# The last pair of step 0: keys and queries made ahead of the products with U, and one buffer for keys and values in both steps

## Chip, cores and metric

The kernel runs on one core of one Trainium2 chip. Its metric is the device time of one execution in microseconds (us), given as the median over several executions. A core has TensorE (PE; its weight loads are shown apart as PEld), VectorE (DVE), ScalarE (ACT), GpSimd (POOL) and SyncE (SP). In this kernel SP only starts transfers, and POOL starts some as well.

## The reference, cut to what matters

There are two layers over N = 2708 rows of D = 512 numbers. The first is graph attention with a dense adjacency matrix. The second spreads features in two steps, and in each step forms an attention matrix that keeps, in each row, the largest entries up to a share of 0.9 of the mass (the nucleus). The change is in the second layer:

```python
def _adj_from_feats(Xa, W1, W2, W3):
    Q = Xa @ W1
    K = Xa @ W3
    logits = Q @ W2 @ K.T / TAU
    ...                                  # keep the nucleus of each row
    return jax.nn.softmax(masked, axis=1)
Xf, Xb, Xa = (X, X, X)
Z = jnp.zeros_like(X)
for s in range(STEPS):                   # STEPS = 2
    A = _adj_from_feats(Xa, W1, W2, W3)
    Xf = Rf @ Xf
    Xb = Rb @ Xb
    Xa = A @ Xa
    Z = Z + (Xf @ U1[s] + Xb @ U2[s] + Xa @ U3[s])
Y = X + Z                                # then a layernorm
```

Step 1 can form no row of its attention before it has keys for every row of the Xa that step 0 made: its keys need the whole of step 0's attention, but nothing of Z, and so nothing of the products with U.

## The kernel before, in words

Rows are cut into 22 tiles of 128 (the last has 20), and tiles are worked in 11 pairs. The first layer fills the time up to about 1074 us, where its last projection ends. Then comes `for s in range(STEPS)`, which opens its pools of buffers anew for each step.

For one pair a step does this. `Logits.products` (L517) multiplies queries with keys, and ACT copies the result out (`p`, L519). ACT takes exponentials, and `search` finds the cut of each row on DVE with passes over whole rows (`L624`, `L800`, `L802`). `attended` turns the kept entries (L1004), copies them (`at`, L1008) and multiplies them with the values `va` (L1023); the result, scaled, is `xa` (L1031). `mixed` then forms the pair's share of Z. It turns the rows of xf, xb and xa (`transposed`, L147, copied to `v_t` by L149) and multiplies them with U1, U2 and U3, in this order, all into two PSUM tiles (L1051). Each of U's twelve pieces `u_k` is loaded by SP (L1049) into three buffers in step 0, so the load of one piece waits for the product three pieces earlier. In step 0 `mixed` calls `project` last: 16 small matmuls (L160) with `kw` give keys and queries of the next step. ACT copies them (L165, L166), POOL splits them in a high and a low part (L170 to L172) and stores them in `kq_d` (L173). At the very end `mixed` adds up Z: ACT copies (`yo`, L1064), POOL adds the old rows (L1068) and stores to `y_d` (L1070).

Between the products of a pair, PE also multiplies pieces of the graph matrix (`part`, L959, with the loads `hl` and `s_r`), so that PE has something to do while DVE searches. For the last pair of a step no such pieces are left.

A step begins with SP loading `keys` from `kq_d` (L924, two loads of 2560 columns and two of 148), then in step 1 `g_b` (L933), and then the queries `q_t` of the first two pairs (L505). Step 1 then calls `ranks`: DVE makes a ramp in a buffer named `s_r` (L1098), PE multiplies it with `keys` (L1103), ACT copies the result to `same` (L1104), PE turns that (L1108), ACT copies columns out (`own`, L1112), and DVE counts with it (L1119). Only then come the first logits of step 1 (L517).

The order of the work on PE, ACT, DVE and SP within a step's main part is written out by hand (`tc.manual_schedule`). The loads of keys and of `g_b` stand outside that part; there a scheduler decides where in SP's queue they go. [...] A pool that is opened where an older one was released makes the first user of its memory wait until the whole older pool is done with:

```python
        with ExitStack() as st:
            big = st.enter_context(tc.tile_pool(name=f"s{s}big", bufs=1))
            ...
            va = big.tile([P, NT, D], F32, name="va")

            keys = big.tile([P, N], F32R, name="keys")
```

Of the kernel before, what the change touches and what calls it, by code (L numbers as in the profile page):

```python
# [9 lines left out]
F32 = mybir.dt.float32  # L10
BF16 = mybir.dt.bfloat16
# [13 lines left out]
P = 128  # L25
# [28 lines left out]
def kernel(  # L54
# [100 lines left out]
    def project(pool, pk, v_t, t, s):  # L155


        pr = rows[t]
        for k in range(KD):
            nc.tensor.matmul(pk[:, :pr], lhsT=kw[:, k, :], rhs=v_t[:, k, :pr], start=(k == 0), stop=(k == KD - 1))  # L160
        big = pool.tile([P, P], F32, name="kq_b")
        hl = pool.tile([P, 2, P], F32, name="kq_hl")
        if pr < P:
            nc.gpsimd.memset(hl, 0.0)
        nc.scalar.copy(hl[:, 1, :pr], pk[:, :pr])  # L165
        nc.scalar.mul(big[:, :pr], pk[:, :pr], 4097.0)  # L166


        high, x = hl[:, 0, :pr], hl[:, 1, :pr]
        nc.gpsimd.tensor_tensor(high, big[:, :pr], x, op=OP.subtract)  # L170
        nc.gpsimd.tensor_tensor(high, big[:, :pr], high, op=OP.subtract)
        nc.gpsimd.tensor_tensor(x, x, high, op=OP.subtract)  # L172
        nc.gpsimd.dma_start(out=kq_d[s][:, :, t * P:(t + 1) * P], in_=hl)  # L173
# [419 lines left out]
    def search(lg, looked, early, late):  # L593
# [307 lines left out]
        v.reciprocal(rden, den)  # L901
        return keep, rden

    for s in range(STEPS):
        last = s == STEPS - 1
        with ExitStack() as st:
            big = st.enter_context(tc.tile_pool(name=f"s{s}big", bufs=1))
            wide = st.enter_context(tc.tile_pool(name=f"s{s}wide", bufs=2))
            sp = st.enter_context(tc.tile_pool(name=f"s{s}sp", bufs=4 if last else 3))
            work = st.enter_context(tc.tile_pool(name=f"s{s}work", bufs=2))  # L910
            up = st.enter_context(tc.tile_pool(name=f"s{s}u", bufs=4))
            parts = None if last else st.enter_context(tc.tile_pool(name=f"s{s}parts", bufs=2))
            small = st.enter_context(tc.tile_pool(name=f"s{s}small", bufs=2))
            ps_t = st.enter_context(tc.tile_pool(name=f"s{s}pst", bufs=2, space=PSUM))
            ps_a = st.enter_context(tc.tile_pool(name=f"s{s}psa", bufs=2, space=PSUM))
            ps_s = st.enter_context(tc.tile_pool(name=f"s{s}pss", bufs=1, space=PSUM))

            va = big.tile([P, NT, D], F32, name="va")

            keys = big.tile([P, N], F32R, name="keys")  # L920
            h = (NT - NT % G - G) * P
            for c in (slice(0, h), slice(h, N)):
                for i in range(2):
                    nc.sync.dma_start(out=keys[i * DA:(i + 1) * DA, c].bitcast(F32), in_=kq_d[s][:DA, i, c])  # L924
            rank = big.tile([P, N], BF16, name="rank") if last else None

            def values():
                for t in range(NT):
                    nc.sync.dma_start(out=va[:rows[t], t, :], in_=(xa_d if last else va_d)[cols[t], :])

            if last:
                g_b = big.tile([P, D], F32, name="g_b")
                nc.sync.dma_start(out=g_b, in_=row_bcast(gamma, D))  # L933

            def part(half, b):
# [101 lines left out]
            def turned_rows(grp, v):  # L1037
                return [transposed(up, ps_t, v[i], rows[t], "v_t") for i, t in enumerate(grp)]

            def mixed(grp, v_t, xb, xa, others, fills):  # L1040

                pz = [ps_a.tile([P, D], F32, name="a") for _ in grp]
                for n, u in enumerate((u1, u2, u3)):
                    nxt = turned_rows(grp, (xb, xa)[n]) if n < 2 else None
                    for k in range(KD):
                        u_k = up.tile([P, D], F32, name="u_k", bufs=4 if last else 3)
                        nc.sync.dma_start(out=u_k, in_=u[s, k * P:(k + 1) * P, :])  # L1049
                        for i, t in enumerate(grp):  # L1050
                            nc.tensor.matmul(pz[i][:rows[t]], lhsT=v_t[i][:, k, :rows[t]], rhs=u_k,  # L1051
                                             start=(n == 0 and k == 0), stop=(n == 2 and k == KD - 1))
                        paced(others, 1)
                        if n < 2 and k < 3:
                            paced(fills, 1)
                    if n == 2 and not last:
                        for i, t in enumerate(grp):
                            project(small, ps_t.tile([P, 512], F32, name="t"), v_t[i], t, s + 1)
                    v_t = nxt
                out_ = []  # L1060
                for i, t in enumerate(grp):
                    pr = rows[t]
                    y = work.tile([P, D], F32, name="yo")
                    nc.scalar.copy(y[:pr], pz[i][:pr])  # L1064
                    z = work.tile([P, D], F32, name="xw", bufs=2) if last else va[:, t, :]
                    if last:
                        nc.sync.dma_start(out=z[:pr], in_=y_d[cols[t], :])
                    nc.gpsimd.tensor_tensor(y[:pr], y[:pr], z[:pr], op=OP.add)  # L1068
                    if not last:
                        nc.gpsimd.dma_start(out=y_d[cols[t], :], in_=y[:pr])  # L1070
                    out_.append((t, y))
                return out_
# [66 lines left out]
            with tc.manual_schedule(engines={PE, ACT, DVE, SP}):  # L1139
                counted, spread = ranks() if last else (None, None)  # L1140
                lg = [Logits(pools, s, grp, keys, rank) for grp in pairs[:1]]
                lg[0].queries()
                lg[0].products()
                steps = lg[0].exp(looks=False)
                if last:
                    counted()
                for step in steps:
                    step()
                half = []
                lg += [Logits(pools, s, grp, keys, rank) for grp in pairs[1:2]]  # L1150
                lg[1].queries()
                for step in part(half, 0):
                    step()
                values()
                done = []
                ready = None
                looks, left = [], []
                for g in range(-1, NP):

                    fills = []  # L1160
                    if g + 2 < NP:
                        lg[g + 2].products()
                    paced(looks, len(looks))
                    if g + 3 < NP:
                        lg.append(Logits(pools, s, pairs[g + 3], keys, rank))
                        lg[g + 3].queries()
                    norms = [normed(t, y) for t, y in done] if last else []
                    done = []

                    rows_in = []  # L1170
                    if g >= 0:
                        left.append(lambda g=g: rows_in.extend(diffused(pairs[g])))
                    others = left + part(half, g + 2)
                    left = []

                    def early(g=g):
                        if g + 2 < NP:
                            fills.extend(lg[g + 2].exp())
                        return lambda: [rest() for rest in norms]

                    def late(g=g):
                        if g >= 0:
                            keep, rden = ready
                            if g:
                                paced(others, 1)
                            xa, v_t = attended(pairs[g], keep, rden, fills, others, lambda: turned_rows(pairs[g], rows_in[0]))
                            done.extend(mixed(pairs[g], v_t, rows_in[1], xa, others, fills))
                            paced(others, len(others))
                            paced(fills, len(fills))
                            return  # L1190


                        if last:
                            spread()
                        paced(fills, 5 + G * NA)
                        paced(others, NT if last else NT - NT // 2)
                        looks.extend(fills)
                        left.extend(others)

                    if g + 1 < NP:  # L1200
                        ready = search(lg[g + 1], g >= 0, early, late)
                    else:
                        for rest in norms:
                            rest()
                        late()
                if last:
                    for rest in [normed(t, y) for t, y in done]:
                        rest()
# [31 lines left out]
```

## Time and profile before

| | us |
|---|---|
| median of 3 runs (3777.3 to 3778.19) | 3777.57 |
| time of the profiled execution | 3774.21 |
| its span, first to last instruction | 3772.1 |
| PE busy | 3383.3 (90%) |
| DVE busy | 2611.1 (69%) |
| ACT busy | 1540.1 (41%) |
| POOL busy | 838.2 (22%) |
| last product with U in step 0 (L1051) ends | 2321.6 |
| first product with the keys of step 1 (L1103) begins | 2338.98 |

The profile is one execution, so times within it are compared with its own span; 2.1 us lie around that span, and the median of the runs shown is 3.4 us over the profiled execution's time. Matmuls overlap and their ends are modelled, so a busy PE isn't yet a PE at its peak. An fp32 product is recorded as two matmuls here: 48 records are the 24 products of one pair with U. A wait for several things is put down to the one that came last.

### The profile page before, as it was taken

Reading aid. Unit: us, or ns where it says so; the run is one execution under the profiler, and the core shown is the slowest. Engines: PE = TensorE matmul, PEld = TensorE weight load, DVE = VectorE, ACT = ScalarE, POOL = GpSimd, SP = SyncE. Lnnn points to the kernel's source line nnn. Section 1 sums busy time; section 2 is a strip of 40 time slices with the busy share of each in tenths; the row PEclk is TensorE's granted clock in tenths of the full one; section 3 lists DMA queues with packets and bytes.
Section 4 is the critical chain, followed back from the end, with each engine's and each line's share of the span. In section 5 each row is a group of like instructions: output and inputs, shape, how many; then the busy total and the mean of one; then the engine's idle time right before and its main releaser. Section 6 shows DMA issues by size and latency. Waiting matters only on the chain. (4 is left out here: it accounts for less than half of the span.)

```text
span 3772.1 us, 35425 instructions
## 1 busy us (share of the span) xinstructions
PE 3383.3 (90%) x11143; PEld 1760.6 (47%) x11143; DVE 2611.1 (69%) x4814; ACT 1540.1 (41%) x2334; POOL 838.2 (22%) x1187
## 2 busy tenths in 40 slices
PE   8999999999855898989898998668999999999988
PEld 4433333333533455545454453435555665556443
DVE  4588888989946526474554641967779798777992
ACT  2343202111025565546566621335544556445511
POOL 4115151423331121121212020302121211212101
PEclk9999999999977999999999998989999999999989
DMA  3476424233154554454545352845556665567552
GB/s 115 159 255 219 155 78 140 85 99 114 44 167 143 193 197 158 154 184 146 195 146 206 114 176 83 302 130 206 187 202 225 229 209 192 197 212 243 184 192 88
DMA packets 276457, 634.07 MB, mean 168 GB/s; under 512 B 37209, under 2 KB 70441, under 8 KB 273243
## 3 DMA queue, kind: packets, MB, share of 16 engines
q1 hardware_dynamic: 249183, 540.99, 43.3%
q0 software_dynamic: 27024, 90.30, 6.3%
q8 instruction: 89, 1.46, 0.2%
q14 instruction: 161, 1.32, 0.1%
HBM read 509.07 MB, written 122.10 MB: 167 GB/s over the span
## 5 line engine op out<-in xcount | busy, mean ns | idle before, releaser
L1023 PE MATMUL a<-va,at 128*128 128x512 f32 (+2 forms) x1936 | 898.0, 603 | 58.0 <-ACT at L1008 57.9
L959 PE MATMUL q<-hl,s_r 128*128 128x512 f32 x2904 | 821.8, 429 | 67.2 <-DMA s_r<-s_d 65.7
L429 PE MATMUL po<-e,fw 128*65 128x512 f32 (+4 forms) x2112 | 840.4, 553 | 30.0 <-DVE e L427 22.2
L427 DVE SCALAR_TENSOR_TENSOR e<-r_b,kk,a_c 128x512 f32<-128x512 f32 (+4 forms) x1056 | 752.3, 741 | 68.8 <-PE po L429 18.2
L959 PEld LDWEIGHTS q<-hl,s_r 128*128 128x128 f32 x2904 | 545.8, 190 | 312.4 <-issue 147.5
L549 ACT ACTIVATE junk_a<-p,nth 128x2708 uint8<-128x2708 f32 (+1 forms) x240 | 613.0, 2554 | 93.2 <-POOL nth L569 89.6
L429 PEld LDWEIGHTS po<-e,fw 128*65 128x65 f32 (+1 forms) x2112 | 286.5, 140 | 544.2 <-issue 269.1
L1023 PEld LDWEIGHTS a<-va,at 128*128 128x128 f32 (+2 forms) x1936 | 339.6, 188 | 428.2 <-issue 347.2
L1051 PE MATMUL a<-u_k,v_t 128*128 128x512 f32 (+1 forms) x1056 | 490.8, 601 | 20.9 <-ACT xa L1031 15.1
L624 DVE SCALAR_TENSOR_TENSOR junk<-p,th 128x2708 bf16<-128x2708 f32 (+1 forms) x132 | 402.2, 3047 | 4.0
L1008 ACT COPY at<-t 128x512 f32<-128x512 f32 (+3 forms) x308 | 139.8, 476 | 439.4 <-PE t L1004 439.2
L1051 PEld LDWEIGHTS a<-u_k,v_t 128*128 128x128 f32 (+1 forms) x1056 | 188.6, 186 | 239.6 <-issue 187.0
L517 PE MATMUL t<-keys,q_t 128*128 128x452 f32 x528 | 167.9, 444 | 117.0 <-ACT p L519 95.0
L800 DVE SCALAR_TENSOR_TENSOR keep<-p,th 128x2708 f32<-128x2708 f32 (+1 forms) x44 | 133.4, 3033 | 132.4 <-PE t L1004 131.1
L181 DVE TENSOR_SCALAR split_hl<-xe 128x512 int32<-128x512 int32 (+1 forms) x44 | 19.0, 432 | 275.6 <-ACT xe L965 232.6
L802 DVE MAX8 vn<-keep 128x8 f32<-128x2708 f32 (+1 forms) x66 | 196.8, 2981 | 2.3
L519 ACT COPY p<-t 128x452 f32<-128x452 f32 (+2 forms) x264 | 132.7, 539 | 149.8 <-DVEq L884 78.9
L517 PEld LDWEIGHTS t<-keys,q_t 128*128 128x128 f32 x528 | 91.8, 211 | 188.7 <-ACT p L519 149.5
L411 ACT ACTIVATE s_c<-a_c 128x512 fp32r<-128x512 f32 (+3 forms) x132 | 76.2, 577 | 248.3 <-DMA a_c<-in_adj_t_dram 123.2
L1004 PE MATMUL t<-ident,keep 128*128 128x128 f32 (+1 forms) x968 | 146.4, 273 | 21.9 <-DVE keep L752 16.5
L1004 PEld LDWEIGHTS t<-ident,keep 128*128 128x128 f32 (+1 forms) x968 | 114.5, 138 | 105.1 <-issue 76.9
L544 DVE TENSOR_REDUCE nmx<-p 128x1 f32<-128x2708 f32 (+1 forms) x44 | 129.2, 2966 | 40.3 <-ACT p L519 40.1
(294 smaller groups left out, 3105.1 us busy)
## 6 DMA issues: line engine op xcount, KB each, us to landing
s_r<-s_d SPq DMA_DIRECT2D x330, 256.0 KB
hl<-vhl_d SPq DMA_DIRECT2D x132, 512.0 KB
u_k<-in_L_gnn_U_dram SPq DMA_DIRECT2D x264, 256.0 KB
hl<-fhl_d SPq DMA_DIRECT2D x132, 512.0 KB
hl<-bhl_d SPq DMA_DIRECT2D x132, 512.0 KB
arow<-in_adj_dram SPq DMA_DIRECT2D x21, 1354.0 KB
s_d<-s_c SPq DMA_DIRECT2D x88, 256.0 KB
a_c<-in_adj_t_dram SPq DMA_DIRECT2D x84, 256.0 KB
```

What stands on the lines that cost most here:

```text
L427: nc.vector.scalar_tensor_tensor(e[:pr, :cw], r_b[:pr, i, :cw], kk[:pr, t, hd:hd + 1], a_c[t][:pr, :cw], op0=OP.max, op1=OP.mult)
L429: nc.tensor.matmul(po[i][:, :cw], lhsT=fw[:pr, t, hd, :], rhs=e[:pr, :cw], start=(t == 0), stop=(t == NT - 1))
L517: nc.tensor.matmul(pl[:, :c1 - c0], lhsT=q[:, i], rhs=self.keys[:, c0:c1], start=(i == 0), stop=(i == 1))
L549: nc.scalar.activation(junk[:pr], self.p[i][:pr], func, **kw)
L624: v.scalar_tensor_tensor(junk_b[:pr], ps_[i][:pr], th, ps_[i][:pr], op0=OP.is_ge, op1=OP.mult, accum_out=dst)
L800: v.scalar_tensor_tensor(keep[i][:pr], ps_[i][:pr], t, ps_[i][:pr], op0=OP.is_lt, op1=OP.mult, accum_out=left[:pr, i:i + 1] if e else None)
L802: v.max(vs, keep[i][:pr])
L959: nc.tensor.matmul(half[j], lhsT=s_r[:, j * P:(j + 1) * P], rhs=hl[:, h], start=(c == 0 and h == 0), stop=(c == NT - 1 and h == 1))
L1004: nc.tensor.transpose(pt[:rows[c], j, :pr], keep[i][:pr, cols[c]], ident[:pr, :pr])
L1008: nc.scalar.copy(at[:r, j0:j1, :pr], pt[:r, j0:j1, :pr])
L1023: nc.tensor.matmul(pa[:pr], lhsT=at[:rows[c], j, :pr], rhs=va[:rows[c], c, :], start=(c == 0), stop=(c == NT - 1))
L1051: nc.tensor.matmul(pz[i][:rows[t]], lhsT=v_t[i][:, k, :rows[t]], rhs=u_k, start=(n == 0 and k == 0), stop=(n == 2 and k == KD - 1))
```

## The change

In step 0, `mixed` gets a flag `final` for the last pair. With it the rows of `xa` are turned first, then `project` is called, and only then do the products with U follow, in the order U3, U1, U2. The turning of xf, which `attended` used to start in place of a next block just before its last product, moves into `mixed`. `va` and `keys` are allocated once, ahead of the loop over the steps, in a pool that both steps use. The other pools of a step now wait tile by tile (`reuse_waits="tile"`): a new tile waits only for those older tiles whose memory it takes. `rank` and `g_b` go to a pool of their own, which is opened in step 1 after the loads of keys and has no such flag.

In the built program the scheduler, free of the old buffer's release, now places SP's loads otherwise. The two large loads of keys stand after the third `u_k` of the last pair, the two small ones after the fourth, and `g_b` and the eight `q_t` between the later `u_k`:

```
u_k u_k u_k  keys keys (2560)  u_k(U3,3)  keys keys (148)  u_k(U1,0)  g_b  u_k(U1,1)  q_t q_t
u_k(U1,2)  q_t q_t q_t  u_k(U1,3)  q_t q_t  u_k(U2,0)  q_t  u_k(U2,1)  u_k(U2,2)  u_k(U2,3)  hl s_r ...
```

On PE, ACT and POOL the order differs from before only in this last pair, and on DVE not at all. The number of instructions is the same on each engine, apart from those that only wait.

```diff
+    big = ctx.enter_context(tc.tile_pool(name="big", bufs=1))
+    va = big.tile([P, NT, D], F32, name="va")
+
+    keys = big.tile([P, N], F32R, name="keys")
     for s in range(STEPS):
         last = s == STEPS - 1
         with ExitStack() as st:
-            big = st.enter_context(tc.tile_pool(name=f"s{s}big", bufs=1))
-            wide = st.enter_context(tc.tile_pool(name=f"s{s}wide", bufs=2))
...
+            wide = st.enter_context(tc.tile_pool(name=f"s{s}wide", bufs=2, reuse_waits="tile"))
...
-            va = big.tile([P, NT, D], F32, name="va")
-
-            keys = big.tile([P, N], F32R, name="keys")
             h = (NT - NT % G - G) * P
             for c in (slice(0, h), slice(h, N)):
                 for i in range(2):
                     nc.sync.dma_start(out=keys[i * DA:(i + 1) * DA, c].bitcast(F32), in_=kq_d[s][:DA, i, c])
-            rank = big.tile([P, N], BF16, name="rank") if last else None
+            if last:
+                also = st.enter_context(tc.tile_pool(name="s1also", bufs=1))
+            rank = also.tile([P, N], BF16, name="rank") if last else None
...
-                g_b = big.tile([P, D], F32, name="g_b")
+                g_b = also.tile([P, D], F32, name="g_b")
...
-            def mixed(grp, v_t, xb, xa, others, fills):
+            def mixed(grp, v_t, xf, xb, xa, others, fills, final=False):
                 pz = [ps_a.tile([P, D], F32, name="a") for _ in grp]
-                for n, u in enumerate((u1, u2, u3)):
-                    nxt = turned_rows(grp, (xb, xa)[n]) if n < 2 else None
+                if final:
+
+                    v_t = turned_rows(grp, xa)
+                    for i, t in enumerate(grp):
+                        project(small, ps_t.tile([P, 512], F32, name="t"), v_t[i], t, s + 1)
+                for n, u in enumerate((u3, u1, u2) if final else (u1, u2, u3)):
+                    nxt = turned_rows(grp, ((xf, xb) if final else (xb, xa))[n]) if n < 2 else None
...
-                    if n == 2 and not last:
+                    if n == 2 and not last and not final:
                         for i, t in enumerate(grp):
                             project(small, ps_t.tile([P, 512], F32, name="t"), v_t[i], t, s + 1)
...
+                            final = g == NP - 1 and not last
+                            xa, v_t = attended(pairs[g], keep, rden, fills, others,
+                                               lambda: None if final else turned_rows(pairs[g], rows_in[0]))
+                            done.extend(mixed(pairs[g], v_t, *rows_in, xa, others, fills, final))
```

More of the change, by code (lines that the diff above doesn't have):

```diff
@@ L906 @@
         with ExitStack() as st:
-            big = st.enter_context(tc.tile_pool(name=f"s{s}big", bufs=1))
-            wide = st.enter_context(tc.tile_pool(name=f"s{s}wide", bufs=2))
[L909 to L916, printed above, removed]
-            va = big.tile([P, NT, D], F32, name="va")
-            keys = big.tile([P, N], F32R, name="keys")
+            wide = st.enter_context(tc.tile_pool(name=f"s{s}wide", bufs=2, reuse_waits="tile"))
+            sp = st.enter_context(tc.tile_pool(name=f"s{s}sp", bufs=4 if last else 3, reuse_waits="tile"))
+            work = st.enter_context(tc.tile_pool(name=f"s{s}work", bufs=2, reuse_waits="tile"))
+            up = st.enter_context(tc.tile_pool(name=f"s{s}u", bufs=4, reuse_waits="tile"))
+            parts = None if last else st.enter_context(tc.tile_pool(name=f"s{s}parts", bufs=2, reuse_waits="tile"))
+            small = st.enter_context(tc.tile_pool(name=f"s{s}small", bufs=2, reuse_waits="tile"))
+            ps_t = st.enter_context(tc.tile_pool(name=f"s{s}pst", bufs=2, space=PSUM, reuse_waits="tile"))
+            ps_a = st.enter_context(tc.tile_pool(name=f"s{s}psa", bufs=2, space=PSUM, reuse_waits="tile"))
+            ps_s = st.enter_context(tc.tile_pool(name=f"s{s}pss", bufs=1, space=PSUM, reuse_waits="tile"))
             h = (NT - NT % G - G) * P
@@ L1185, in late @@
                                 paced(others, 1)
-                            xa, v_t = attended(pairs[g], keep, rden, fills, others, lambda: turned_rows(pairs[g], rows_in[0]))
-                            done.extend(mixed(pairs[g], v_t, rows_in[1], xa, others, fills))
+                            final = g == NP - 1 and not last
+                            xa, v_t = attended(pairs[g], keep, rden, fills, others,
+                                               lambda: None if final else turned_rows(pairs[g], rows_in[0]))
+                            done.extend(mixed(pairs[g], v_t, *rows_in, xa, others, fills, final))
                             paced(others, len(others))
```

## The prediction

> **What bounds the kernel now.** I read the page first. PE is busy for 90% of the span, DVE for 69%:
>
> ```profile
> span 3772.1 us, 35425 instructions
> PE 3383.3 (90%) x11143; PEld 1760.6 (47%) x11143; DVE 2611.1 (69%) x4814; ACT 1540.1 (41%) x2334; POOL 838.2 (22%) x1187
> PEclk9999999999977999999999998989999999999989
> ```
>
> The page's chain is no help: it holds only the last 1.2 us. So I looked for the place of the change, the passage from step 0 to step 1, and took the list of waits from 2296 to 2357 us. Columns: who waited for whom, total us, times, longest.
>
> ```profile
> DVE s_r L1098 <- DMA y_d<-yo: 82.2, 1, 82.2
> ...
> PE t L1103 <- DMA keys<-kq_d: 15.4, 1, 15.4
> ...
> DVE junk L1119 <- ACT own L1112: 4.9, 1, 4.9
> ```
>
> PE stands still for 15.4 us for the keys. DVE has nothing to do for 82.2 us, so its wait costs nothing by itself. The timeline of PE around it (start, duration, line, operation, count):
>
> ```profile
> 2293.53 2.00 PE L1023 MATMUL a<-va,at 128*20 128x512 f32 x4
> 2295.46 1.01 PE L147 MATMUL t<-ident,x 128*128 128x128 f32 x8
> 2296.39 8.15 PE L1051 MATMUL a<-u_k,v_t 128*128 128x512 f32 x16
> 2304.48 1.00 PE L147 MATMUL t<-ident,xa 128*128 128x128 f32 x8
> 2305.41 16.24 PE L1051 MATMUL a<-u_k,v_t 128*128 128x512 f32 x32
> 2321.58 1.96 PE L160 MATMUL t<-v_t,kw 128*128 128x128 f32 x16
> 2338.98 1.09 PE L1103 MATMUL t<-keys,s_r 128*128 128x452 f32 x2 [15.44 <-DMA keys<-kq_d]
> ```
>
> PE has no gap until 2323.54; the keys' own matmuls come last. SP's timeline shows what then stands in a row:
>
> ```profile
> 2298.51 17.43 SPq L1049 DMA_DIRECT2D u_k<-in_L_gnn_U_dram  x9
> 2329.89 2.44 SPq L924 DMA_DIRECT2D keys<-kq_d  x4
> 2332.37 0.58 SPq L933 DMA_DIRECT2D g_b<-in_L_gnn_gamma_dram  x1
> 2333.12 8.18 SPq L505 DMA_DIRECT2D q_t<-kq_d  x8
> ```
>
> ACT's last projection copy ends at 2323.89, POOL splits and adds rows until 2329.86, the loads of keys start at 2329.89 and land some 9 us later. That is the gap. The granted clock falls in it (column before the DMA share):
>
> ```profile
> 2306.00:2324.00 18.00, 17.54 (x48) 4.88 (x46) 0.00 (x0) 0.82 (x5) 0.45 (x1) 1.00 0.27 86
> 2324.00:2339.00 15.00, 0.02 (x1) 0.05 (x1) 2.15 (x2) 0.82 (x2) 6.36 (x11) 0.62 0.62 153
> 2339.00:2356.00 17.00, 15.40 (x55) 10.46 (x56) 11.61 (x24) 9.63 (x25) 0.00 (x0) 0.73 0.51 166
> ```
>
> After the gap the path is DVE's: `own` releases it at 2344.45, and it then works until the end of the first search near 2500 us with only a few waits of 1 to 2 us, while PE multiplies with S at 296 GB/s of loads. Whatever moves L1103 moves this whole start of step 1.
>
> **What the Trainium skill says.** "DMA: Bandwidth & Descriptors", section "Anatomy of one DMA — SWDGE (gpsimd) path", gives about 2.0 us fixed plus bytes over 436 GB/s: 2.3 us for a 128 KB store of `kq_d`. The trace agrees: 2.2 and 2.3 us from issue to landing. The same page, "Issuing engines are not separate DMA queues", says that all issuers' transfers interleave on the same 16 engines. So loads moved under the products with U share with `u_k`; the trace shows room, a DMA share of 0.27 there. "TensorE: Matmul & The Clock Gate", Part 1, says that an idle window of about 3.4 us halves PE's clock; the means of 0.62 and 0.73 above fit that, with both clocks in one window.
>
> **The change part by part.** Same instructions, in another order; times are those of the profiled execution (span 3772.1, time 3774.21).
>
> (1) PE's order in the last pair. From 2292.59 to the first product with U, PE now does the last attention products (1.93, start to start), turning xa (0.93), projecting (1.96) and turning xf (0.93): 5.75, so 2298.3. Turning xb (0.93) moves between the products; the sum of PE's work doesn't change. New are short waits, because xa is needed at once: ACT must copy xa (0.68) while PE turns the first tile's rows (about 0.6), then `v_t` (0.59) before PE projects, and both projections must be copied out (0.27 + 0.28 and 0.18 + 0.19) before xf may take their PSUM buffers. Walking through it I get 2299.0, 0.7 over the sum. Bounds: 0.3 and 2.
>
> (2) Keys and queries. The second projection is copied out near 2298.3. POOL needs 1.6 to split (as at 2323.89 to 2325.4), 0.3 and two issues of 0.7; its addition to `yo` (1.26), which stood between, is now later. The last store starts at 2300.9 and lands at 2303.2. Before it started at 2327.2.
>
> (3) SP's queue. The two large loads of keys wait only for the stores of the pair before (the last is issued at 2255.25) and start near 2258, where the DMA share is soon 0.03: free, hidden under attention. The two small ones now stand ahead of `u_k`(U1,0) and wait for 2303.2. Behind them: the rest of the `u_k`, and so PE. Issues are 0.6 each, so `u_k`(U1,0) starts at 2304.5. Products with U3 take 8.15 from 2299.0, turning xb 0.93: it is needed at 2308.1, 3.6 later. From there each `u_k` may be issued when the product three pieces earlier is done, 6.1 before it is needed (3 x 2.03); in between stand up to three `q_t` of 0.6 (1.8). 4 us remain for the issue and landing of 256 KB. No row gives the landing of `u_k`; POOL's stores of that size need 2.3 to 3.0. In the pair before, a slack of 5.2 (3 x 1.74) was enough with no stall. I take 1.0 in all; bounds 0 (no stall) and 6 (nine loads late by 0.7).
>
> (4) Sum. Products with U end at 2299.0 + 8.15 + 0.93 + 16.24 + 1.0 = 2325.3. Keys, ramp (DVE idle, its new wait is for loads before 2250) and PSUM are there, so L1103 begins at 2325.3 in place of 2338.98: **13.7 us gained**. `g_b` waits for ACT's and POOL's work on the projections (about 2300), already past. POOL's additions now lie beside L1103; ACT's `yo` copies (0.6 each) can delay the third copy of `same` by up to 0.5, and the full clock in place of 0.62 to 0.73 gives about that back. I take 0 for both together; bounds -0.5 and 2.
>
> (5) The rest of the tile-wise waits, and the passage from layer 1 to step 0: nothing. There PE waits 20.0 us for `q_t`, behind keys whose last store leaves POOL only at 1086.91; that order is untouched. Stores named in the new waits landed long before. A cost or gain of 1 either way can't be excluded.
>
> (6) Does it reach the end? DVE, PE and the loads of step 1 all hang on L1103 or on SP being free (`hl` issued near 2320 in place of 2341.56), in the same order as before; nothing there is tied to an absolute time. So the shift should last: 3772.1 - 13.7 = 3758.4 span; 3777.57 - 13.7 = **3763.9** against the median.
>
> **The rivals.**
> B, crowding on SP: `q_t`, `g_b` and the wait for the last store push the `u_k` so that PE starves. For it: eight `q_t` took 8.18 before, 1.02 each with their waits. Then three between two `u_k` eat 3.1 of 6.1. Stall about 6 (nine times 0.7): gain 8, 3769.6. Against it: those waits were for the large loads of keys in front, which are now gone.
> C, given back: the start moves, but step 1's start has a second limit, the products with S at 296 GB/s. If that stream starts no earlier than about 2352 in effect, a gain of 3 at most, 3774.6. Against it: SP is free earlier, and DVE is the later one.
> D, slower: SP's queue becomes serial with the products. If each of nine `u_k` comes 1.5 late (13.7 / 9), all is lost; at 2.4 late (21.3 / 9) it is 7.6 slower. It needs landings of about 6.5 where 4 are to be had. For it: waits in SP's queue also wait for the eighth transfer back. Time 3785. Against it: a DMA share of 0.27 and slack in the pair before.
> E, the change doesn't do what it says, as the small loads of keys wait for the end of the step after all: then about the old gap plus the waits of (1), 3777 to 3779. The built order and its waits speak against it; I count it with C.
>
> **How the numbers follow.** Main case 0.72, B 0.16, C and E 0.07, D 0.05. Within the main case (1) can cost 1.3 more or 0.4 less, (3) up to 2 more or 1.0 less, (4) 0.5 more or 2 less, (5) 1 either way; they seldom add up, so a gain of 11 to 16, 3761.5 to 3766.6. For 8 in 10 I reach down to 3760.5 for (4), and up to 3769.0, over half of B. A measurement can tell 0.2%, 7.6 us, from no change: 3770.0 and 3785.1 are the limits. Faster: 0.72 + 0.15 of B = 0.87. Same: 0.08. Slower: 0.05.
>
> **What would show it.** Right: the wait of PE at L1103 for keys is gone or under 1 us, L1103 begins near 2325, `own` releases DVE near 2330, large loads of keys start before 2270, and the clock stays near 1.00 from 2324 to 2356. Step (3) is wrong if L1051 shows waits for `u_k` of over 1 us in sum in this pair, (1) if the first product with U begins after 2300. (6) is wrong if L1103 moves by 13 and the span by much less.

## The result and the profile after

| | before | changed |
|---|---|---|
| median of 5 runs each, us | 3777.57 | 3759.38 |
| lowest and highest | 3777.25, 3778.97 | 3750.71, 3761.9 |
| time of the profiled execution | 3774.21 | 3750.71 |
| its span | 3772.1 | 3748.9 |

The ratio is 0.9946, with a 95% interval of 0.9936 to 0.9957: 18.2 us less, where 13.7 were forecast. The profiled execution of the changed kernel is the fastest of its five, so its span alone would flatter the change. From the page of the changed kernel:

```profile
span 3748.9 us, 35397 instructions
PE 3377.5 (90%) x11143; PEld 1759.3 (47%) x11143; DVE 2612.2 (70%) x4814; ACT 1540.2 (41%) x2334; POOL 836.7 (22%) x1187
PEclk9999999999977899999999999889999999999999
```

The sums are close to those of before. PE's busy time is 6 us less with the same number of instructions, so most of the 23 us of span is waiting that has gone, and its place has to be looked up. PE's timeline around the change (start, duration, line, operation, count, in brackets the wait ahead of it):

```profile
2280.45 5.43 PE L1025 MATMUL a<-va,at 128*20 128x512 f32 x12
2285.81 0.66 PE L147 MATMUL t<-ident,xa 128*128 128x128 f32 x4
2287.14 1.96 PE L160 MATMUL t<-v_t,kw 128*128 128x128 f32 x16
2289.86 8.15 PE L1058 MATMUL a<-u_k,v_t 128*128 128x512 f32 x16
2299.43 2.09 PE L1058 MATMUL a<-u_k,v_t 128*128 128x512 f32 x4 [0.47 <-DMA u_k<-in_L_gnn_U_dram]
2302.26 14.22 PE L1058 MATMUL a<-u_k,v_t 128*128 128x512 f32 x28 [0.75 <-DMA u_k<-in_L_gnn_U_dram]
2316.41 0.68 PE L1110 MATMUL t<-keys,s_r 128*128 128x452 f32 x2
2319.78 2.69 PE L1115 MATMUL t<-ident,keep 128*128 128x128 f32 x22 [0.19 <-ACT keep L1111]
```

(Lines have moved by two to nine: L1025 was L1023, L1058 was L1051, L1110 was L1103, L1115 was L1108, L1126 was L1119.) L1110 follows the last product with U without a gap, where PE stood for 15.4 us. But the first row already starts 8.6 us earlier than before (2289.05), ahead of anything that this pair does differently. So two amounts must be kept apart. I measure the **passage** from the last copies of `at` in step 0 to DVE's first use of `own`, in one view of all engines:

```profile
2280.61 0.23 ACT L1010 COPY at<-t 128x20 f32<-128x20 f32 x2 [3.50 <-PE t L1006]
...
2320.66 0.35 DVE L1126 SCALAR_TENSOR_TENSOR junk<-keep,own 128x128 bf16<-128x128 f32 x1 [71.63 <-ACT own L1119]
```

That is 40.05 us. The same places before, from the timelines of PE, ACT and DVE, with PE's row that gave the 8.6:

```profile
2289.05 3.61 PE L1023 MATMUL a<-va,at 128*20 128x512 f32 x8
...
2289.21 0.23 ACT L1008 COPY at<-t 128x20 f32<-128x20 f32 x2 [3.50 <-PE t L1004]
...
2344.45 0.35 DVE L1119 SCALAR_TENSOR_TENSOR junk<-keep,own 128x128 bf16<-128x128 f32 x1 [4.89 <-ACT own L1112]
```

That is 55.24 us. The passage gained **15.2 us**. SP's timeline of the changed kernel shows how (some rows):

```profile
2249.33 1.11 SPq L924 DMA_DIRECT2D keys<-kq_d  x2
2291.99 0.33 SPq L1056 DMA_DIRECT2D u_k<-in_L_gnn_U_dram  x1
2295.41 1.08 SPq L924 DMA_DIRECT2D keys<-kq_d  x2
2296.59 0.54 SPq L1056 DMA_DIRECT2D u_k<-in_L_gnn_U_dram  x1
2297.29 0.33 SPq L935 DMA_DIRECT2D g_b<-in_L_gnn_gamma_dram  x1
2297.72 0.38 SPq L1056 DMA_DIRECT2D u_k<-in_L_gnn_U_dram  x1
...
2310.83 0.43 SPq L955 DMA_DIRECT2D hl<-fhl_d  x1
```

The large loads of keys start 40 us ahead of the products with U (2249.33 to 2289.86), and the small ones under them. SP is held for 3.0 us until 2295.41, when the last store of keys and queries has landed. The first load of the next stage (`hl`) starts at 2310.83, or 2319.43 with the 8.6 us added back; before it started at 2341.56. The list of waits over this stretch (who for whom, total us, times, longest):

```profile
DVE junk L1126 <- ACT own L1119: 71.6, 1, 71.6
...
PE a L1058 <- DMA u_k<-in_L_gnn_U_dram: 1.2, 2, 0.7
...
PE t L1110 <- ACT keep L1111: 0.7, 2, 0.5
```

No wait of PE for keys is left, and none of DVE for `y_d`. The granted clock in the same three stretches as before, moved by 8.6 us (clock, then DMA share and GB/s at the end):

```profile
2297.40:2315.40 18.00, 16.78 (x40) 3.94 (x38) 0.00 (x0) 0.71 (x2) 0.00 (x0) 1.00 0.71 214
2315.40:2330.40 15.00, 13.11 (x57) 7.62 (x57) 9.28 (x19) 10.50 (x27) 3.66 (x4) 1.00 0.30 115
2330.40:2347.40 17.00, 13.53 (x55) 9.64 (x54) 16.82 (x15) 11.21 (x11) 1.80 (x2) 1.00 0.78 247
```

1.00 stands where 0.62 and 0.73 stood. The loads have moved under the products with U: 214 GB/s there in place of 86.

### The profile page after: what moved, and what is told of

Read it like the earlier page. It is cut to its first block, busy times and chain, and to the rows that moved or that the text cites. A ratio compares the mean times of both kernels' runs of the same rounds, so it can differ in the third digit from the quotient of the medians.

```text
span 3748.9 us, 35397 instructions
## 1 busy us (share of the span) xinstructions
PE 3377.5 (90%) x11143; PEld 1759.3 (47%) x11143; DVE 2612.2 (70%) x4814; ACT 1540.2 (41%) x2334; POOL 836.7 (22%) x1187
## 5 line engine op out<-in xcount | busy, mean ns | idle before, releaser
L1025 PE MATMUL a<-va,at 128*128 128x512 f32 (+2 forms) x1936 | 898.0, 603 | 57.9 <-ACT at L1010 57.7
L427 DVE SCALAR_TENSOR_TENSOR e<-r_b,kk,a_c 128x512 f32<-128x512 f32 (+4 forms) x1056 | 750.9, 740 | 64.9 <-PE po L429 13.8
L1025 PEld LDWEIGHTS a<-va,at 128*128 128x128 f32 (+2 forms) x1936 | 339.9, 188 | 428.5 <-issue 347.2
L1058 PE MATMUL a<-u_k,v_t 128*128 128x512 f32 (+1 forms) x1056 | 490.2, 601 | 22.0 <-ACT xa L1033 14.7
L1058 PEld LDWEIGHTS a<-u_k,v_t 128*128 128x128 f32 (+1 forms) x1056 | 188.8, 186 | 240.0 <-issue 185.6
```

The lines of the kernel that those rows point to most:

```text
L427: nc.vector.scalar_tensor_tensor(e[:pr, :cw], r_b[:pr, i, :cw], kk[:pr, t, hd:hd + 1], a_c[t][:pr, :cw], op0=OP.max, op1=OP.mult)
L1025: nc.tensor.matmul(pa[:pr], lhsT=at[:rows[c], j, :pr], rhs=va[:rows[c], c, :], start=(c == 0), stop=(c == NT - 1))
```

## The experiments

### Where do the other 8.6 us come from?

Both kernels were run again, unchanged, for a second trace of each.

Before again:

> The kernel before once more, unchanged, for a second trace of it. Two theories on the 8.6 us by which the changed kernel's trace leads before the last pair of step 0 is reached (2.4 us arise in the first layer, where no line is changed; 0.8 at the passage from layer 1 to step 0; 3.4 near the search of the third pair at 1640 to 1690 us; 2 more from 2040 to 2220 us). Theory 'chance': two executions of one and the same kernel drift apart by such amounts, because small waits for transfers fall differently. Then this trace stands 2 to 6 us away from the first trace of before when the last pair begins, most likely later, since the first trace (3774.21) was 3.4 us under the median of before. Theory 'tile waits': the waits of the pools cost before 3 to 6 us in the searches of step 0, in every execution. Then this trace agrees with the first one within 1.5 us up to the last pair. Both expect 3777.6 +- 1 as the median.

Changed again:

> The changed kernel once more, unchanged, for a second trace of it. Both theories expect the passage from step 0 to step 1 to gain 15.2 +- 0.5 us again (from the last attention product of step 0, L1025, to the first use of own by DVE, L1126), against the first trace of before. Theory 'chance' expects the lead at 2280 us to be another than 8.6, anywhere from 0 to 8, and the end 24 us minus that difference ahead; theory 'tile waits' expects a lead of 7 to 9.5 at 2280 us again, 4 of it at the third pair's search. Median near 3759, single times over 10 us.

Measured: before again has a median of 3780.6 over 21 executions (3772.62 to 3787.66), beside 3778.07 over 36 (3771.25 to 3784.92): a ratio of 1.0006, from 1.0000 to 1.0013, for one and the same kernel. The changed kernel again has 3761.86 (3755.92 to 3763.03), a ratio of 0.9955 (0.9942 to 0.9969). A third sample of it, beside the last two kernels below, has 3760.41 and 0.9951 (0.9938 to 0.9965):

> The changed kernel a third time, beside the two that follow. Passage (last copies of `at` in step 0 to DVE's first use of `own`) 40.0 +- 0.2; median 13 to 18 us under before's of the same chip, and single times spread over 10 us or more, for reasons outside the passage.

The traces are cut at the same two places of the passage, read from ACT's and DVE's timelines (us). The table has kernels that are told of below too; the last two experiments have their figures there.

| kernel | start to the last `at` copies | passage | from `own` to the end |
|---|---|---|---|
| before | 2289.21 | 55.24 | 1427.64 |
| before again | 2283.91 | 55.07 | 1431.56 |
| tile-wise waits in step 0 only | 2289.93 | 55.06 | 1429.25 |
| order alone | 2287.55 | 52.68 | 1433.47 |
| shared buffer, no tile-wise waits | 2289.19 | 46.81 | 1432.41 |
| pools alone | 2286.89 | 44.91 | 1429.90 |
| changed | 2280.61 | 40.05 | 1428.27 |
| changed again | 2287.38 | 39.91 | 1432.80 |
| changed, third trace | 2289.50 | 39.89 | 1429.08 |
| tile-wise waits in step 1 only | 2286.01 | 39.77 | 1431.74 |
| four `u_k` | 2284.09 | 38.69 | 1433.29 |

The passage comes back within 0.2 us. The two other columns do not: they spread over 9 and 6 us, and traces of one kernel differ by up to 5.3 (before) and 8.9 (changed) in the first. Before again leads the first trace of before by 5.3 us when the last pair begins (I had expected it to be later; it was earlier). Of this, 2.2 us arise near the third pair's search, where the first trace of before was the slow one. The changed kernel again leads the first trace of before by 1.8 us, where the theory 'tile waits' expected 7 to 9.5. So the 8.6 us are for the most part the drift of single executions, as the theory 'chance' has it. Two more kernels show whether the tile-wise waits have a part in it.

Tile-wise waits in step 0 alone, on the kernel before:

```diff
+        tw = {} if last else {"reuse_waits": "tile"}
...
-            wide = st.enter_context(tc.tile_pool(name=f"s{s}wide", bufs=2))
+            wide = st.enter_context(tc.tile_pool(name=f"s{s}wide", bufs=2, **tw))
...
```

> The kernel before with tile-wise waits in the pools of step 0 only; nothing else is changed. Both theories expect a passage of 55.2 +- 0.3. Theory 'tile waits' (they bring 2 to 3 us at the start of step 0 or in its searches, the part of the changed kernel's gain of 18 that lies outside the passage's 15.2): median 3775 to 3776, time from the first row maximum of step 0 (DVE L544) to the last copies of `at` 1184 to 1186. Theory 'chance': the median within 2.5 us of before's, on either side, and that time anywhere from 1184 to 1190, as in the traces so far (1189.45 and 1185.02 in two traces of before, 1184.21 and 1185.47 in two of the changed kernel).

Tile-wise waits in step 1 alone, on the changed kernel:

```diff
+        tw = {"reuse_waits": "tile"} if last else {}
...
-            wide = st.enter_context(tc.tile_pool(name=f"s{s}wide", bufs=2, reuse_waits="tile"))
+            wide = st.enter_context(tc.tile_pool(name=f"s{s}wide", bufs=2, **tw))
...
```

> The changed kernel with tile-wise waits in the pools of step 1 only; step 0's pools wait as in before. Both theories expect the passage at 40.0 +- 0.3. Theory 'tile waits': 2 to 3 us of the gain are lost, median 3762 to 3765. Theory 'chance': as the changed kernel, 3757 to 3763.

Measured: 3776.36 beside 3775.88 for the first (ratio 1.0007, 0.9999 to 1.0016): step 0's tile-wise waits bring nothing by themselves. From the first row maximum of step 0 to the last copies of `at` it takes 1189.7 us, outside the 1184 to 1186 of the theory 'tile waits'. The second has 3762.99 beside the same 3775.88 (0.9965, 0.9953 to 0.9976), 12.9 us under before, with the passage untouched at 39.77. That median alone lies in the range of both theories; but the four-buffer kernel below, which has the waits in both steps, gained no more on the same chip (13.8). Nothing here speaks for step 0's waits as the source of the 8.6 us.

### What the 15.2 us are made of

Pools alone, the last pair in its old order:

```diff
-                            final = g == NP - 1 and not last
+                            final = False
```

> The changed pools alone: keys and values in one buffer for both steps and tile-wise waits, but the last pair in the old order, with its projection last. The large loads of keys start early, near 2250 us; only the two small ones (37 KB each) wait for the last stores of keys and queries, which land near 2329.5 on before's clock. They are issued then and land some 2.5 us later, so L1110 begins near 2332.5 in place of 2338.98: 6.5 us gained at the passage, between 5 and 8. PE still waits some 9 us there for keys and its clock still falls. Theory 'tile waits' adds the 3 to 6 us of the searches of step 0: median 3765 to 3768. Theory 'chance': 3769 to 3772.5.

Measured: passage 44.91, so 10.3 us are gained where 6.5 were expected; median 3765.52, ratio 0.9966 (0.9956 to 0.9977). That median lies in the range of 'tile waits', but both ranges were set with 6.5. With 3.8 less, for the 10.3, it lies in that of 'chance' (3765.2 to 3768.7) and above that of 'tile waits' (3761.2 to 3764.2). PE's timeline has the reason for the 10.3:

```profile
2321.07 1.02 PE L1110 MATMUL t<-keys,s_r 128*128 128x452 f32 x2
2322.98 0.90 PE L1110 MATMUL t<-keys,s_r 128*128 128x452 f32 x2 [0.89 <-ACT keep L1111]
2324.08 0.50 PE L1110 MATMUL t<-keys,s_r 128*128 128x452 f32 x1 [0.21 <-ACT keep L1111]
2330.01 0.71 PE L1110 MATMUL t<-keys,s_r 128*128 128x448 f32 x1 [5.42 <-DMA keys<-kq_d]
```

Five of the six pieces need only the large loads, which are there. They and their copies are done before the small loads land. Only the last piece waits, nearly to the time I had named for all of them, 2332.5 (2330.01 plus this trace's lead of 2.3 us is 2332.3).

The order alone, with before's pools (edit against the changed kernel, in part):

```diff
-    big = ctx.enter_context(tc.tile_pool(name="big", bufs=1))
...
+            big = st.enter_context(tc.tile_pool(name=f"s{s}big", bufs=1))
-            wide = st.enter_context(tc.tile_pool(name=f"s{s}wide", bufs=2, reuse_waits="tile"))
+            wide = st.enter_context(tc.tile_pool(name=f"s{s}wide", bufs=2))
...
```

> The order of the last pair alone: keys and queries made ahead of the products with U, but with before's pools, each step its own. In the built order all loads of keys and queries of step 1 then stand behind the release of step 0's pools, thus behind the landing of the last store to y_d, and the eight loads of q_t are in front of those of keys. I expect the products with U to end near 2322.5 on before's clock, y_d to land near 2328, eight q_t to take 5, the keys to land 8 later: L1103 near 2341, 2 us later than before, between 1 earlier and 5 later. PE waits some 18 us for keys. Median 3776.5 to 3782.5 by both theories, since this kernel has no tile-wise waits. If it gains over 3 us, the early projection is of use by itself, and my reading of the waits is wrong.

Measured: 3776.49, ratio 0.9997 (0.9988 to 1.0005): no change that can be told. The passage is 52.68, 2.6 less than before, where I had allowed 1 at most. SP's timeline:

```profile
2302.26 1.17 SPq L505 DMA_DIRECT2D q_t<-kq_d  x2
...
2325.99 2.38 SPq L924 DMA_DIRECT2D keys<-kq_d  x4
```

I had put the eight `q_t` behind the release of the pools. They go out between the `u_k`; only the keys wait, for POOL's last addition to `yo` (its end is 2325.97). The keys are in DRAM some 23 us earlier than they may be loaded: the first `q_t`, which reads from the same stores, goes out at 2302.26. PE waits 12.0 us for the keys. This is what rival E described, loads of keys that wait for the end of the step after all: without the shared buffer the early projection is worth 2.6 us.

The shared buffer and the order, without tile-wise waits:

```diff
-            wide = st.enter_context(tc.tile_pool(name=f"s{s}wide", bufs=2, reuse_waits="tile"))
+            wide = st.enter_context(tc.tile_pool(name=f"s{s}wide", bufs=2))
...
```

> The changed kernel with the one buffer for keys and values and the new order of the last pair, but without tile-wise waits in the steps' pools. The measure is the passage: from the start of the last copies of `at` in step 0 (ACT, L1010) to DVE's first use of `own` (L1126). It is 55.24 and 55.07 us in two traces of before, 40.05 and 39.91 in two of the changed kernel, 44.91 with the pools alone, 52.68 with the order alone. Here the loads of keys stand as early as in the changed kernel, but DVE's ramp (L1105) waits for the whole of step 0, so for the landing of the second store to y_d, some 6 us behind the end of the products with U. Theory 'all three parts count': PE's L1110 waits for the ramp, passage 46 to 49, and PE's clock falls in the gap; median near 3770. Rival 'the shared buffer is enough': passage 40 to 41, median near 3761.

Measured: passage 46.81, median 3770.19, ratio 0.9982 (0.9973 to 0.9992). From its list of waits:

```profile
DVE s_r L1105 <- DMA y_d<-yo: 76.6, 1, 76.6
...
PE t L1110 <- DVE s_r L1105: 5.7, 1, 5.7
```

DVE's ramp waits for the landing of the last `y_d`, and PE now waits for the ramp. In the trace of before DVE's 82.2 us wait for `y_d` cost nothing, because the keys were later still. With the keys early it ends last. The passage lies in the range that was named for 'all three parts count' (46 to 49). So all three parts count: early keys in DRAM, a buffer that may take them, and a ramp that doesn't wait for step 0. Pools alone and order alone give 10.3 + 2.6 = 12.9; together they give 15.2. A kernel with tile-wise waits but without the shared buffer was not run; that the buffer counts is read from the order alone, where the keys wait for its release.

### Is SP crowded?

Four buffers for `u_k` in step 0:

```diff
-                        u_k = up.tile([P, D], F32, name="u_k", bufs=4 if last else 3)
+                        u_k = up.tile([P, D], F32, name="u_k", bufs=4)
```

> The changed kernel with four buffers for u_k in step 0 in place of three, so that each u_k may be loaded one product earlier. In the changed kernel PE waits 0.47 and 0.75 us for u_k in the last pair (0.53 and 0.46 in its second trace), behind the small loads of keys, which hold SP's queue until the last store of keys has landed. Theory 'queue': the first u_k of U1 now starts ahead of that wait, these PE waits fall under 0.4 us in sum, passage 39.0 +- 0.3. Rival 'transfers': the u_k land late because loads share the DMA engines; then PE's waits stay near 1 us and the passage at 40.0. In the other pairs of step 0 nothing waits for u_k, so the median moves by no more than 1 us from this, under what can be told.

Measured: median 3762.08 (0.9969, 0.9956 to 0.9981). PE's timeline:

```profile
2302.37 16.24 PE L1058 MATMUL a<-u_k,v_t 128*128 128x512 f32 x32
2318.54 0.67 PE L1110 MATMUL t<-keys,s_r 128*128 128x452 f32 x2
```

The products with U1 and U2 run through, 16.24 us as before the change, and the passage is 38.69, some 1.3 shorter than in the changed kernel, as the theory 'queue' expected. But a fourth buffer gives each load one product (2.03 us) more time, and that would cover slow transfers too, so by itself it doesn't part the theories. SP's rows of the changed kernel help. The buffer of the first `u_k` of U1 came free when the second product with U3 was done, that of the second one product later: 2293.9 and 2296.0, estimated as 2289.86 plus 2 and 3 times 2.03. They went out at 2296.59 and 2297.72, so 2.7 and 1.8 us late, behind the small loads of keys. That is more than the 0.47 and 0.75 us that PE waited for them, so by this estimate PE would not have waited without the hold. The transfers have a part in the second wait: that `u_k` took 4.5 us from issue to first use, the other 2.8. The gain of 1.3 us is under what the medians can tell.

### Does an earlier start always reach the end?

In the changed kernel the last keys are loaded from 2295.41 on, the products with U end near 2316.5, and DVE idles for 71.6 us until `own`. The first kernel below uses such keys 4.0 us after the issue of their last loads, without a wait for them. Two kernels take the products with U1 and U2 out of the way, first behind the first logits of step 1 (edit in part):

```diff
+                if final:
+                    xf_t = turned_rows(grp, xf)
+                    times(0, u3, v_t)
+                    xb_t = turned_rows(grp, xb)
...
+                    def products():
+                        times(1, u1, xf_t)
+                        times(2, u2, xb_t)
...
+                    owed.extend((products, summed))
+                    return []
...
                 lg[0].products()
...
+                if last:
+                    owed[0]()
```

> The changed kernel taken further. The keys of step 1 are there some 17 us before PE is done with the products with U, and DVE idles for 70 us until `own`. So only U3's products of the last pair stay ahead; those with U1 and U2 (16.2 us of PE) move behind the ramp's products, the turning and the first pair's logits of step 1. Their PSUM buffers and the turned rows get pools that both steps use. PE's L1110 should begin near 2299 on the changed kernel's clock in place of 2316.4: passage 22.5, between 21 and 25. What that is worth at the end: theory 'DVE bounds the start of step 1' expects nearly all of it, 15 to 17 us under the changed kernel. Rival 'the products with S bound it': their stream still begins only when the products with U are done, and DVE waits for the second pair's logits instead; PE had 7.5 us to spare there (wait for p, in the trace of the changed kernel), so 3 to 8 us under the changed kernel.

and then behind the second pair's logits (edit in part; the old rows for Z are loaded anew there):

```diff
                         lg[g + 2].products()
+                    if last and g < 0:
+                        owed[0]()
...
+                            owed[1]()
                             spread()
```

> As the one before, but the products with U1 and U2 stand still later: behind the first block of products with S and the second pair's logits of step 1, where PE waits 8.4 us for S in the changed kernel. The old rows for Z are loaded anew, since va is overwritten by then. Passage as there, 22.5. The stream of products with S begins some 17 us earlier too. Theory 'the start of step 1 is bound by DVE and that stream together': 17 less 8 to 10 for products with U that PE can't hide behind its wait: 6 to 15 us under the changed kernel, and 3 or more under the kernel before this one in the list. Rival: eight loads of u_k (2 MB, some 7 us at the 296 GB/s of that stream) push the S loads back and eat it: within 3 us of the one before.

Measured for the first: passage 23.64, 16.3 less than the 39.9 of the changed kernel, but a median of 3759.07 beside its 3760.41 (ratio to before 0.9948, 0.9935 to 0.9962). The list of waits shows where it went:

```profile
DVE nmx L544 <- ACT p L519: 16.7, 2, 15.4
```

DVE waits 15.4 us for the second pair's logits; in the changed kernel it was 1.4. Those stand on PE behind the first block of products with S (L964), and that block begins when the products with U end:

```profile
2319.88 16.14 PE L1060 MATMUL a<-u_k,v_t 128*128 128x512 f32 x32
2335.95 2.14 PE L964 MATMUL q<-hl,s_r 128*128 128x512 f32 x8
```

That is 49.5 us after the last copies of `at` (2286.42), as in the changed kernel, where it is 49.4:

```profile
2329.98 5.65 PE L961 MATMUL q<-hl,s_r 128*128 128x512 f32 x24
...
2402.53 0.28 PE L1132 MATMUL t<-ident,rk 128*22 128x128 f32 x1
2411.20 10.37 PE L961 MATMUL q<-hl,s_r 128*128 128x512 f32 x32 [8.39 <-DMA s_r<-s_d]
```

From `own` to the end this kernel takes 1447.1 us, 14 to 19 more than the traces of the changed kernel. This is the rival "given back", and here it is true.

For the second: passage 23.37, median **3748.86** (3745.22 to 3750.61), ratio to before 0.9915 (0.9901 to 0.9928). PE's timeline:

```profile
2321.03 5.60 PE L964 MATMUL q<-hl,s_r 128*128 128x512 f32 x24
...
2396.36 16.14 PE L1060 MATMUL a<-u_k,v_t 128*128 128x512 f32 x32
2412.42 0.28 PE L1153 MATMUL t<-ident,rk 128*22 128x128 f32 x1
2422.86 10.20 PE L964 MATMUL q<-hl,s_r 128*128 128x512 f32 x32 [10.16 <-DMA s_r<-s_d]
```

The products with S begin at 2321, right after the first logits, 33.6 us after the last copies of `at` and not 49.4. DVE's wait for the second pair's logits is 3.9 us. The products with U now stand where the changed kernel waited 8.4 us for S. They don't fill that wait, though: PE still waits 10.2 us for S behind them, and the second block with S begins 135.4 us after the copies of `at`, in the changed kernel 130.6. The rows show why. In both kernels the loads of S for this block stand in SP's queue behind the store of the ranks (`rank_d`), which needs PE's turning of `rk` (L1132 in the changed kernel, L1153 here), and that turning now stands behind the products with U. The store goes out at 2413.28 and the first of these loads at 2415.72; the eight loads of `u_k`, which the rival of this run's expectation blamed, are all issued by 2404.76. From `own` to the end it takes 1438.0 us: of the 16.5 us that the passage gained beside the changed kernel, 5 to 10 are lost again in this trace. By the medians this kernel beats both others: it is 11.5 us under the changed one on the same chip.

## Why the prediction was right or wrong

Its own steps, against the changed kernel's first trace, with 8.60 us added to its times:

- (1) PE's order. First product with U at 2289.86, so 2298.46; I had 2299.0. The waits for ACT came to 0.2 us and not 0.7. Right in kind, 0.5 too dear.
- (2) Keys and queries. POOL's two stores are issued from 2291.13 to 2292.56. The second landed 3.6 us after its issue and not 2.3, so near 2304.0; I had 2303.2. The large loads start at 2249.33, so 2257.9; I had 2258. Right, but the price of 2.3 us held only for the first store (2.2).
- (3) SP's queue: 1.2 us of waits for `u_k`; I had 1.0. The other two traces of the changed kernel have 1.0 and 1.1. The sign that I had named for a wrong step, over 1 us, is met in two of three traces, by 0.2 at most. The hold of SP's queue was there as described. Rival B's 6 us were not there, nor D.
- (4) The sum. L1110 at 2316.41, so 2325.01; I had 2325.3, with the errors of (1) and (3) partly against each other. The last term of this sum was mis-sized: "I take 0 for both together", for the copies and for the clock. From L1110 to `own` it took 4.25 us (4.34 in the second trace) where before took 5.47. PE's products there are shorter at the full clock (0.68, 0.91 and 0.91 us in place of 1.09, 1.18 and 1.18); the one longer wait for a copy (0.49 in place of 0.25) took little of it back. This lay within the bound, but not in the number: 13.7 + 0.3 + 1.2 = 15.2.
- (5) "Nothing", with 1 us either way, for all the rest. This is the step that failed. The passage's 15.2 us alone would give 3777.57 - 15.2 = 3762.4, inside the range; the medians have 3.0 us more. Stretches that the change doesn't touch differ by 4 to 9 us between traces of one kernel. As a mean effect nothing contradicts "nothing"; as a bound on what one reads in a few executions, 1 us was wrong.
- (6) The shift lasts. Yes: from `own` to the end the changed kernel's three traces take 1428.3, 1432.8 and 1429.1, before's two 1427.6 and 1431.6. The reason given was right: DVE's start and the stream of products with S moved together. Where only DVE's start moved (the products with U behind the first logits), 15 of 16 us were lost.

Then the range. It was made of the bounds of the passage and that 1 us, on the footing of three runs within 0.9 us. That these lay so close was chance: 36 further executions of before lie between 3771.25 and 3784.92. The measured 3759.38 lies 1.1 us under my lower end, 3760.5.

Three medians of the changed kernel (3759.38, 3761.86, 3760.41), each beside the median of before measured with it (3777.57, 3778.07, 3779.53), give gains of 18.2, 16.2 and 19.1. What they have above the passage's 15.2, 1 to 4 us, was not located, and no stretch of the traces shows it steadily. It is no sure property of the change: one kernel differed from itself by 2.5, and on a further chip the kernels with the waits in step 1 only and with four `u_k` gained 12.9 and 13.8, which is less than their passages' 15.5 and 16.6. So medians of so few executions lie up to 3 or 4 us on either side of what the passage gives, and where that comes from stays open.

## What to carry to other kernels

When a wait is removed, look for the next thing behind the same instruction: here early keys without a buffer that takes them gained 2.6 us at the passage, and with it but with a ramp that waits for the old step, 8.4. Before moving an engine's start, ask which two streams must meet after it, and move both: with DVE's start alone 1.3 of 16.3 us reached the end. And cut the traces at fixed instructions on both sides of the change: a stretch of 40 us came back within 0.2 us, while whole times of one kernel spread over 13.

## What the runs showed of the hardware beyond that

The clock can fall without a long pause of PE. The turning of `same` (L1115, 22 transposes) took 2.69 us in the first and third traces of the changed kernel, and in the second:

```profile
2326.30 4.29 PE L1115 MATMUL t<-ident,keep 128*128 128x128 f32 x22 [0.19 <-ACT keep L1111]
```

The mean clock of the 15 us from 2322 on is 0.89 there, and 1.00 in the other two. Yet PE's longest wait in the 30 us ahead is 0.53 us there, and 0.75 and 0.84 in the other two. The Trainium skill, "TensorE: Matmul & The Clock Gate", Part 1, says that the activity window runs freely, so that one kernel shows different clocks from run to run; these three traces agree. It also says that the low clock follows an idle window of about 3.4 us; no such pause is in this trace. Whether the short waits or the turning itself bring the fall isn't shown. `own` came no later for it (4.34 us after L1110, beside 4.25), since its first use needs only the first group of turned columns.
